# A two-layer relational graph attention kernel: the last eight products of layer 1 by column half, and the third part of W2 loaded in halves around them

## The chip, the cores and the metric

The kernel runs on one core of a Trainium2 chip. The core has a matrix engine (TensorE, in the profile PE, with its weight loads as PEld), a vector engine (VectorE, DVE), an engine for activations and copies (ScalarE, ACT), a general engine (GpSimd, POOL), and an engine that here only issues transfers (SyncE, SP). Sixteen DMA engines move data between the chip's memory (HBM) and the on-chip buffer (SBUF). SP, ACT and POOL each issue transfers on a queue of their own: SP the plain loads and stores, ACT the loads of W2, POOL the indirect gathers. Each engine works through its instructions in order, so an instruction that waits holds everything behind it on that engine.

The metric is device time in microseconds (us), the median of several runs. The profile is of one execution.

## The reference

Two layers of a relational graph attention network over 3125 nodes with 768 features and 53,125 edges sorted by target, with three relations; then a residual and a layer norm. Layer 1 has four heads, layer 2 one.

```python
def rgat_conv(x, W, q, k, b, src, dst, etype, heads, out_ch, n_nodes):
    xr = jnp.einsum('nd,rdf->rnf', x, W)
    oi = xr[etype, dst]
    oj = xr[etype, src]
    alpha = jax.nn.leaky_relu(oi @ q + oj @ k, NEG_SLOPE)
    m = jax.ops.segment_max(alpha, dst, num_segments=n_nodes)
    e = jnp.exp(alpha - m[dst])
    z = jax.ops.segment_sum(e, dst, num_segments=n_nodes)
    a = e / (z[dst] + EPS)
    msg = (a[:, :, None] * oj.reshape(-1, heads, out_ch)).reshape(-1, heads * out_ch)
    return jax.ops.segment_sum(msg, dst, num_segments=n_nodes) + b

h = jax.nn.elu(rgat_conv(x, W1, q1, k1, b1, src, dst, edge_type, 4, 192, n))
out = _layernorm(x + rgat_conv(h, W2, q2, k2, b2, src, dst, edge_type, 1, 768, n))
```

## The kernel before

The 3125 nodes are cut into 25 blocks of 128 (`NB` = 25, the last one partly empty), the 768 features into six tiles of 128 (`DT`) and two column halves of 384 (`HALF`). Products are made at full float32 precision from parts: each operand is split in a high and a low part, and three products (high by high, high by low, low by high) are added, so a block, a relation and a column half take 6 x 3 = 18 matrix products. The weights' parts lie in two buffers, `wH` and `wL`, of 18 feature tiles (three relations by six) by 770 columns: 384 columns of the first half, two more columns for attention, and 384 of the second half (`HW` = 386 is where the second half begins when they hold W2). The same buffers first hold W1 and then W2.

There are three phases and a preparation, in one hand-written order: the code's order is each engine's order, and only data and buffers make engines wait for one another.

**Phase 1** (`phase1`, L520) makes the products of layer 1 and the attention weights of all edges. Its steps n run over a list of 144 groups, a group being one block, one relation and one column half: 18 products by `d_group` (L688) into one of two `po` buffers of PSUM. `d_row` (L707) follows in the next step: ACT copies the group's result into a row buffer, and when both column halves are there, SP stores the row (128 x 772 numbers, 386 KB) into the table `tab1` in HBM. The row buffers are `share[0]` to `share[2]`, in turn. The first 120 groups go block by block (1 to 20); the last 24, for the blocks 21 to 24, go relation by relation, so that of each relation's weights the last reader comes early. In each relation the order is block by block, both halves of a block behind one another. So the groups 136 to 143 are relation 2 (the third), blocks 21 to 24, two halves each.

Beside the products, the edges' attention runs in steps that are tied to n: for every block, POOL issues 17 indirect gathers (tile `kt`, `a_gather`), and DVE, ACT and TensorE turn them into weights (`a_alpha` to `a_put`); the last block's steps lie behind the last product. W2 is also split into its parts in phase 1 (`w_split`) and written to HBM (`w2_d`).

`second_weights` (L508) brings one third (one relation) of W2 from `w2_d` into `wH` and `wL`, in four loads of 1152 KB on ACT's queue, each one column half of one buffer, and then fills the two attention columns with two small DVE instructions. It is a generator: each `next` issues one load, and the fifth one the DVE instructions. The thirds 0 and 1 are loaded in phase 1, at the steps m = 9 to 12 and 17 to 20, where m = n - 120. The third 2 is loaded in phase 2, since phase 1's last products still read W1 there.

**Phase 2** (`phase2`, L826) gathers `tab1`'s rows per edge, adds them up per node, and makes the products of layer 2. Its steps k run over the edge slots: `gather(k)` has POOL gather 128 rows (386 KB) into one of 14 buffers (`share[0]` to `share[8]` and five `g`); `high` makes the weighted selection masks on DVE (`selp`, L854); `sums` (L858) multiplies masks and rows on TensorE (`acc`, L876), for the first block in seven small batches and for all others in two. Behind a block's sums come its activation (`e_first` for the first block, `e_y`, `e_x`, `e_h` for the others), its transposition and split (`e_t`, `e_s`, `e_s2`: tile `hT`, L928 to L941), and its 18 `d_part` pieces of six products (L953) for three relations and two column halves, between the next block's sums; `d_row` (L956) copies and stores them into `tab2`. The third part of W2 is loaded at the steps 19, 20, 23 and 26, and its DVE instructions stand at step 28.

**Phase 3** (`phase3`, L1016) gathers `tab2`'s rows, and makes layer 2's attention, sums, residual and layer norm. Its gathers start when phase 2 has stored its last rows.

Of the kernel before, what the change touches and what calls it, by code (L numbers as in the profile page):

```python
# [54 lines left out]
def kernel(  # L55
# [21 lines left out]
    R = layers[0]["W"].shape[0]  # L77
    E = src.shape[0]
    NB = (N + P - 1) // P
# [4 lines left out]
    H1 = l1["H"]  # L84
    F1 = D // H1
# [5 lines left out]
    CW = F1 + 1  # L91
    LL = FRONT + E + BACK
    NK = (NB - 1) * SL + SLF
    V, S, G, T = nc.vector, nc.scalar, nc.gpsimd, nc.tensor
# [406 lines left out]
    def x_load(pre, b, to=None):  # L501
        n = min(P, N - b * P)
        xs[b] = pre.tile([P, D], F32, name="xr", bufs=1) if to is None else to[:, :D]
        if n < P:
            V.memset(xs[b], 0.0)
        nc.sync.dma_start(xs[b][:n], x[b * P:b * P + n, :])

    def second_weights(r, wH, wL):  # L508

        i = slice(r * DT, (r + 1) * DT)  # L510
        w = w2_d[r * DT * P:(r + 1) * DT * P, :].rearrange("(i p) (s c f) -> p s i c f", p=P, s=2, c=2)
        for c in range(2):
            for s, o in ((0, wH), (1, wL)):
                nc.scalar.dma_start(o.bitcast(F32)[:, i, c * HW:c * HW + HALF], w[:, s, :, c])
                yield
        V.tensor_copy(wH[:, i, HALF:HW], wkq2[:, i])
        V.tensor_sub(wL[:, i, HALF:HW], wkq2[:, i], wH[:, i, HALF:HW].bitcast(F32))


    def phase1(pre, work, psum, wH, wL, qq):  # L520
# [4 lines left out]
        rows = share[:3]  # L525
# [144 lines left out]
        def d_turn(b):  # L670
            xr = xs.pop(b)
            xt[b] = work.tile([P, 2, DT, P], F32R, **spare.get(b, dict(name="xT", bufs=2)))
            pt = psum.tile([P, 2, 512], F32, name="px", bufs=1)
            for t in range(DT):
                T.transpose(pt[:, t // 3, (t % 3) * P:(t % 3 + 1) * P], xr[:, t * P:(t + 1) * P], ident)
            p3 = pt[:, :, :3 * P]
            st["x", b] = xr, p3
# [25 lines left out]
            st["po", b, r, c] = po  # L703

        n_rows = []

        def d_row(b, r, c):  # L707
            po = st.pop(("po", b, r, c))
            if c == 0:
                n_rows.append(b)  # L710
            o = rows[len(n_rows) % 3]
            to = o.rearrange("p (h f) -> p h f", h=H1)[:, 2 * c:2 * c + 2, :F1]
            S.copy(to, po[:, :HALF].rearrange("p (h f) -> p h f", h=2))  # L713
            if c == 1:
                nc.sync.dma_start(
                    tab1[b * P * R:(b + 1) * P * R, :].rearrange("(p r) f -> p r f", r=R)[:, r, :], o)
                if b == 1:

                    nc.sync.dma_start(tab2[N * R:, :].rearrange("(p r) f -> p r f", r=R)[:, r, :], o)
# [53 lines left out]

        GB = NB - 4
        groups = [(b, r, c) for b in range(1, GB) for r in range(R) for c in range(2)]
        groups += [(b, r, c) for r in range(R) for b in range(GB, NB) for c in range(2)]
        ev = {}

        chain = ((-6, a_index), (-6, a_index2), (-5, a_gathers), (-5, a_next), (-4, a_next2))
# [12 lines left out]
        for b in range(2, GB + 1):  # L792
            for d, f, o in ((-8, d_turn, 0), (-7, d_split, 0), (-7, x_next, 1)):
                ev.setdefault(6 * b + d, []).append((f, NB - 1 if f is x_next and b == GB else b + o))
        for n in range(max(ev) + 1):
            for f, b in ev.get(n, ()):
                f(b)
            b, i = divmod(n, 6)
            if n == 2:
                nc.sync.dma_start(share[3][:, :D], x[:P, :])  # L800
            if n == 8:
                V.tensor_add(share[4][:, :D], share[3][:, :D], b2r)
                nc.sync.dma_start(xb_d[:P, :], share[4][:, :D])
            m = n - 6 * (GB - 1)
            if m in (1, 3, 5):
                d_turn(GB + 1 + m // 2)
                d_split(GB + 1 + m // 2)

            if m in (-8, -3):
                x_load(pre, GB + 1 + (m + 8) // 5, share[6 if m == -8 else 3])  # L810
            if m in (9, 17):
                w2s = second_weights(m // 16, wH, wL)
            if 9 <= m < 25:
                next(w2s, None)
            if 2 <= b < 2 + R * DT:
                if i == 0:
                    w_load(b - 2)
                if i == 2:
                    w_split(b - 2)
            if n < len(groups):  # L820
                d_group(n, *groups[n])
            if 0 < n <= len(groups):
                d_row(*groups[n - 1])


    def phase2(work, psum, wH, wL):  # L826
        bias1 = work.tile([P, D], F32, name="fbias1", bufs=1)
        nc.sync.dma_start(bias1, l1["b"][None, :].to_broadcast([P, D]))
        last_w2 = second_weights(R - 1, wH, wL)
        gs = share + [work.tile([P, RW], F32, name=f"g{i}", bufs=1) for i in range(5)]  # L830
        NG = len(gs)
        rows = [work.tile([P, RW], F32, name=f"r2_{i}", bufs=1) for i in range(3)]
# [148 lines left out]
        for i, b in enumerate(order):  # L981
# [5 lines left out]
            for m in range(6 * R):  # L987
                rc = divmod(m // 3, 2)
                k = e + m * SL // (6 * R) if i else first + 5 + m * (SL + 3) // (6 * R)
# [4 lines left out]
        for k in range(max(ev) + 1):  # L994
            if k < NK:
                gather(k)
            if k in (19, 20, 23, 26, 28):
                next(last_w2, None)
            if 0 <= k - LAG < NK:
                sums(k - LAG)  # L1000
            if k == first:
                e_first(order[0])
            if 0 <= k - LAG + 2 < NK:
                high(k - LAG + 2)
            for f, a in ev.get(k, []):
                f(*a)
            if k == NK + LAG:
                for b in range(len(xbs)):
                    x_load3(b)
# [299 lines left out]
    with tc.manual_schedule():  # L1309
        with tc.tile_pool(name="share", bufs=1) as pool:  # L1310
            share = [pool.tile([P, RW], F32, name=f"share{i}") for i in range(9)]

            two = pall.rearrange("p b j h -> p (b j h)")
            xbs = [t[:, :D] for t in share] + [two[:, i * D:(i + 1) * D] for i in range(2)]
            with tc.tile_pool(name="wbuf", bufs=1) as wbuf:
                wH = wbuf.tile([P, R * DT, D + 2], F32R, name="wH")
                wL = wbuf.tile([P, R * DT, D + 2], F32R, name="wL")
                with tc.tile_pool(name="pre", bufs=1) as pre:
                    qq = pre.tile([P, NB, H1, R], F32, name="qq")
                    with tc.tile_pool(name="work0", bufs=1) as work, tc.tile_pool(  # L1320
                        name="psum0", bufs=1, space=PSUM
                    ) as psum:

                        bank = psum.tile([P, 512], F32, name="bank")
                        bits = prepare(work, bank, share[8], share[6].bitcast(BF))

                        def more(n):
                            for _ in range(n):
                                next(bits, None)

                        buf = Buffers()
                        buf.go()
                        kqr = work.tile([P, DT, 2, H1], F32, name="kqr", bufs=1)
                        for s, name in ((0, "k"), (1, "q")):
                            nc.scalar.dma_start(kqr[:, :, s, :], l1[name].rearrange("(t p) h -> p t h", p=P))
                        more(1)
                        wk, kqs = (work.tile([P, DT, P], F32R, name=n) for n in ("wk", "kqs"))

                        def edges_ready():
                            more(100)  # L1340
                            a_load(pre, 0)

                        turns = nodes_kq(buf, pre, work, psum, bank, wk, kqs, wH, wL, qq, more, edges_ready)
                        weights_kq(buf, work, psum, bank, kqr, wk, kqs, wH, wL, next(turns), more)
                        next(turns)
                    with tc.tile_pool(name="work1", bufs=1) as work, tc.tile_pool(
                        name="psum1", bufs=1, space=PSUM
                    ) as psum:
                        phase1(pre, work, psum, wH, wL, qq)
                with tc.tile_pool(name="work2", bufs=1) as work, tc.tile_pool(name="psum2", bufs=1, space=PSUM) as psum:  # L1350
                    phase2(work, psum, wH, wL)
            with tc.tile_pool(name="work3", bufs=1) as work, tc.tile_pool(name="psum3", bufs=1, space=PSUM) as psum:
                phase3(work, psum)
    return nc.values_load(flag, min_val=0, max_val=1 << 24)
# [537 lines left out]
```

## Time and profile before

| what | value |
|---|---|
| runs | 2060.18 us median of 3 (2058.1 to 2061.2) |
| the profiled execution | 2060.05 us |
| its span, first to last instruction | 2058.3 us |
| mean granted TensorE clock | 0.915 |
| PE busy | 1761.5 us (86%) |
| POOL busy | 1327.4 us (64%) |
| DVE busy | 1185.0 us (58%) |
| ACT busy | 374.1 us (18%) |
| layer 1's last product ends (phase 1) | about 681 us |
| first row gather of phase 2 is issued | 693.92 us |
| phase 2's last product ends | about 1471.4 us |

Times inside the execution are microseconds from the start of the span. An engine's busy time counts what it computes, not what it waits for and not the issuing of transfers; those of ACT and SP are shown as ACTq and SPq. "Releaser" is what ended a wait. The chain that ended last is followed back from the last instruction of the program: at each step to what released it, or to the instruction before it on its engine. Idle time of an engine costs nothing unless it lies on that chain.

### The profile page before, as it was taken

Reading aid. Unit: us, or ns where it says so; the run is one execution under the profiler, and the core shown is the slowest. Engines: PE = TensorE matmul, PEld = TensorE weight load, DVE = VectorE, ACT = ScalarE, POOL = GpSimd, SP = SyncE. Lnnn points to the kernel's source line nnn. Section 1 sums busy time; section 2 is a strip of 40 time slices with the busy share of each in tenths; the row PEclk is TensorE's granted clock in tenths of the full one; section 3 lists DMA queues with packets and bytes.
Section 4 is the critical chain, followed back from the end, with each engine's and each line's share of the span. In section 5 each row is a group of like instructions: output and inputs, shape, how many; then the busy total and the mean of one; then the engine's idle time right before and its main releaser. Section 6 shows DMA issues by size and latency. Waiting matters only on the chain.

```text
span 2058.3 us, 41812 instructions
## 1 busy us (share of the span) xinstructions
PE 1761.5 (86%) x15027; PEld 1482.8 (72%) x15027; DVE 1185.0 (58%) x4163; ACT 374.1 (18%) x659; POOL 1327.4 (64%) x1326
## 2 busy tenths in 40 slices
PE   6989998999999579999999999999666766776775
PEld 5979998899899368988898888888523433433433
DVE  6545554555454456776677667666356556556654
ACT  5421211222111011111111111111102112112111
POOL 4257777777777745556555655564277777777773
PEclk9999999999999889999999999999877777787787
DMA  7655554555547687778777877876699999999993
GB/s 194 192 140 167 176 189 139 172 160 180 176 153 233 216 311 252 258 264 286 250 264 271 279 261 257 280 267 206 223 313 329 343 339 330 339 328 320 320 328 133
DMA packets 156844, 506.31 MB, mean 246 GB/s; under 512 B 43875, under 2 KB 57069, under 8 KB 156628
## 3 DMA queue, kind: packets, MB, share of 16 engines
q0 software_dynamic: 81904, 331.52, 48.2%
q1 hardware_dynamic: 62926, 156.02, 21.8%
q10 hardware_dynamic: 11798, 16.00, 2.3%
q8 instruction: 122, 2.00, 0.4%
q14 instruction: 94, 0.77, 0.1%
HBM read 412.55 MB, written 95.69 MB: 247 GB/s over the span
## 4 chain that ended last, share of the span: by engine, by line
PE 55%; issue 15%; POOL 14%; DMA 10%; DVE 5%; ACT 1%; POOLq 0%; ACTq 0%; DVEq 0%; SPq 0%
PE po L953 23%; PE acc L876 11%; POOL kt L462 11%; PE acc L1147 10%; PE po L698 4%; DMA G<-ftab,ridx 4%; POOL G L462 3%; DMA kt<-kt,ridx 2%; DMA wL<-w_d 2%; PE bank L285 1%; PE pt L263 1%; PE po L395 1%; PE pt L928 1%; DVE F L1107 1%; PE bc L1054 1%
## 5 line engine op out<-in xcount | busy, mean ns | idle before, releaser
L953 PE MATMUL po<-wH,hT 128*128 128x386 f32 (+1 forms) x1800 | 486.7, 345 | 8.5 <-DMA wH<-w_d 5.9
L462 POOL DMA_INDIRECT kt<-kt,ridx x374 | 395.5, 1057 | 114.0 <-issue 110.9
L698 PE MATMUL po<-wH,xT 128*128 128x384 f32 x1584 | 440.6, 348 | 9.7 <-ACT share L713 4.4
L462 POOL DMA_INDIRECT G<-ftab,ridx x374 | 374.2, 1001 | 114.0 <-issue 91.2
L854 DVE TENSOR_SCALAR selp<-frow,fdl,pall 128x32 f32<-128x32 f32 (+1 forms) x1688 | 381.1, 322 | 0.0
L953 PEld LDWEIGHTS po<-wH,hT 128*128 128x128 f32 x1800 | 331.7, 190 | 24.4 <-issue 21.0
L462 POOL DMA_INDIRECT share<-ftab,ridx x239 | 238.4, 997 | 169.8 <-PE acc L876 125.6
L953 PE MATMUL po<-wL,hT 128*128 128x386 f32 (+1 forms) x900 | 306.7, 341 | 4.8 <-DMA wL<-w_d 4.8
L698 PEld LDWEIGHTS po<-wH,xT 128*128 128x128 f32 x1584 | 294.7, 192 | 15.4 <-ACT share L713 6.2
L1147 PE MATMUL acc<-G,selp 128*32 128x386 f32 x2388 | 290.0, 582 | 2.9 <-DVE selp L1133 1.5
L698 PE MATMUL po<-wL,xT 128*128 128x384 f32 x792 | 270.3, 341 | 0.0
L1147 PEld LDWEIGHTS acc<-G,selp 128*32 128x32 f32 x2388 | 178.3, 128 | 77.3 <-issue 45.9
L462 POOL DMA_INDIRECT g<-ftab,ridx x135 | 135.7, 1005 | 108.3 <-PE acc L876 83.0
L876 PE MATMUL acc<-share,selp 128*32 128x193 f32 x3208 | 185.3, 330 | 2.7 <-DMA share<-ftab,rfirst 1.3
L961 ACT COPY r<-po 128x386 f32<-128x386 f32 (+1 forms) x150 | 72.3, 482 | 592.9 <-PE po L953 581.6
L953 PEld LDWEIGHTS po<-wL,hT 128*128 128x128 f32 x900 | 171.3, 190 | 5.2 <-DMA wL<-w_d 5.2
L1060 DVE TENSOR_SCALAR sT<-bc,cols 128x512 bf16<-128x512 f32 (+1 forms) x125 | 83.4, 667 | 150.6 <-PE bc L1054 147.9
L876 PEld LDWEIGHTS acc<-share,selp 128*32 128x32 f32 x3208 | 125.7, 111 | 44.0 <-issue 7.7
L698 PEld LDWEIGHTS po<-wL,xT 128*128 128x128 f32 x792 | 151.7, 191 | 0.0
L1054 PE MATMUL bc<-d,one 1*128 1x512 bf16 (+1 forms) x125 | 48.5, 388 | 85.2 <-DVE sT L1060 82.1
L713 ACT COPY share<-po 128x384 f32<-128x384 f32 x144 | 67.8, 477 | 275.2 <-PE po L698 268.2
L876 PE MATMUL acc<-g,selp 128*32 128x193 f32 x1768 | 115.0, 328 | 1.6 <-DMA g<-ftab,rfirst 1.2
(262 smaller groups left out, 1911.5 us busy)
## 6 DMA issues: line engine op xcount, KB each, us to landing
ftab<-share SPq DMA_DIRECT2D x75, 386.0 KB
ftab<-r SPq DMA_DIRECT2D x75, 386.0 KB
share<-in_L_gnn_W_dram SPq DMA_DIRECT2D x36, 384.0 KB
w_d<-w2hl SPq DMA_DIRECT2D x18, 768.0 KB
sT<-dr_d SPq DMA_DIRECT2D x25, 544.0 KB
share<-in_x_dram SPq DMA_DIRECT2D x27, 384.0 KB
xb_d<-share SPq DMA_DIRECT2D x25, 384.0 KB
xr<-in_x_dram SPq DMA_DIRECT2D x21, 384.0 KB
```

Source lines behind the costliest of these rows:

```text
L263: T.transpose(pt[:, f, c * P:(c + 1) * P], a[:, (2 * i + f) * P:(2 * i + f + 1) * P], ident)
L285: T.matmul(to, a[:, 2 * i + f, :], t[:, f, :w], start=(n == 0), stop=(n == 2 * DT - 1))
L462: return G.indirect_dma_start(out=to, out_offset=None, in_=tab, in_offset=_index(i[:, j:j + 1]), bounds_check=NP * R - 1, oob_is_err=False)
L698: m = T.matmul(po[:, :HALF], xT[:, s, t, :], w[:, i, sl], start=(n == 0), stop=(n == 3 * DT - 1))
L713: S.copy(to, po[:, :HALF].rearrange("p (h f) -> p h f", h=2))
L854: V.tensor_scalar(sel[:, h, :hi - lo], row[:, lo:hi], dl[:, b, j:j + 1], pall[:, b, j, h:h + 1], op0=ALU.is_equal, op1=ALU.mult)
L876: T.matmul(acc[32 * t:32 * t + 32, h // 2, c], sel[:, h, 32 * (t - WINDOW[i][0]):][:, :32], g[:, h * CW:(h + 1) * CW], start=(i == u[0] an ...
L953: T.matmul(po[:, :wd], hT[:, k, t, :], w[:, r * DT + t, sl], start=(t == 0 and n == 0), stop=(t == DT - 1 and n == 2))
L961: S.copy(o[:, c * HW:c * HW + wd], po[:, :wd])
L1054: T.matmul(bc[:, :n], one, s["d"][:, 4 * i * P:4 * i * P + n], start=True, stop=True)
L1060: V.tensor_scalar(s["sT"][:, 4 * i * P:4 * i * P + n], bc[:, :n], cols[:, b:b + 1], None, op0=ALU.is_equal)
L1147: T.matmul(acc[32 * t:32 * t + 32, c, :HW], st[b, j][:, 32 * (t - WINDOW[j][0]):][:, :32], gs[:, (base(b) + j) % NG, c * HW:(c + 1) * HW], ...
```

## The change

The last eight groups, 136 to 143, are put in another order: first the first column half of the blocks 21, 22, 23 and 24, then the second half of the four. For that, four rows are open at once, and the fourth one (block 24) gets `share[3]`, whose four columns of ones are set by a small DVE instruction.

The four loads of W2's third part, which overwrite the weights these groups read, move from phase 2 into phase 1: the first column half of `wH` and of `wL` at m = 21 and m = 22, that is behind the copies of groups 139 and 140 on ACT; the second half of both behind the copy of group 143, the last one. The two DVE instructions of the attention columns move from step 28 of phase 2 to step 19.

```diff
         n_rows = []
+        row_of = {}
 
         def d_row(b, r, c):
             po = st.pop(("po", b, r, c))
             if c == 0:
                 n_rows.append(b)
-            o = rows[len(n_rows) % 3]
+                row_of[b, r] = rows[len(n_rows) % 3] if (b, r) != (NB - 1, R - 1) else share[3]
+                if (b, r) == (NB - 1, R - 1):
+                    V.memset(share[3].rearrange("p (h f) -> p h f", h=H1)[:, :, F1:CW], 1.0)
+            o = row_of[b, r]
...
         groups = [(b, r, c) for b in range(1, GB) for r in range(R) for c in range(2)]
-        groups += [(b, r, c) for r in range(R) for b in range(GB, NB) for c in range(2)]
+        groups += [(b, r, c) for r in range(R - 1) for b in range(GB, NB) for c in range(2)]
+        groups += [(b, R - 1, c) for c in range(2) for b in range(GB, NB)]
...
+        last_w2 = second_weights(R - 1, wH, wL)
         for n in range(max(ev) + 1):
...
             if 9 <= m < 25:
                 next(w2s, None)
+            if m in (21, 22):
+                next(last_w2)
...
             if 0 < n <= len(groups):
                 d_row(*groups[n - 1])
-
-
-    def phase2(work, psum, wH, wL):
+            if n == len(groups):
+                next(last_w2)
+                next(last_w2)
+        return last_w2
+
+
+    def phase2(work, psum, wH, wL, last_w2):
...
-        last_w2 = second_weights(R - 1, wH, wL)
...
-            if k in (19, 20, 23, 26, 28):
+            if k == 19:
                 next(last_w2, None)
...
-                        phase1(pre, work, psum, wH, wL, qq)
+                        last_w2 = phase1(pre, work, psum, wH, wL, qq)
...
-                    phase2(work, psum, wH, wL)
+                    phase2(work, psum, wH, wL, last_w2)
```

## The prediction

> **What bounds the kernel now.** The profiled execution took 2060.05 us, of which 2058.3 are the span; the median of the runs is 2060.18, so sums made against 2060.05 stand 0.13 below it. I read the chain that ended last first, in order of time, around the end of layer 1's products (about 680 us) and the start of phase 2:
>
> ```profile
> 704.35 5.79 DMA share<-ftab,rfirst
> 710.86 4.56 DMA g<-ftab,rfirst
> 721.93 42.87 DMA wL<-w_d
> 768.10 5.64 PE po L953 x30
> ...
> 786.50 5.39 PE acc L876 x100
> 791.89 5.47 PE po L953 x30
> ...
> 798.11 5.29 PE po L953 x30
> 803.40 4.08 PE acc L876 x96
> ```
>
> Columns: start, length, what. Row gathers lead to about 720; then one transfer, a piece of W2, holds the chain for 42.87 us; after that TensorE's own work follows without a hole, and windows of 100 us from 800 to 1400 show PE busy 100.00 at clock 1.00. So a microsecond won before 768 is kept to the end of phase 2, and phase 3's gathers start when that ends. What the load costs TensorE is in its timeline:
>
> ```profile
> 753.12 0.34 PE L953 MATMUL po<-wH,hT 128*128 128x386 f32 x1
> 759.37 0.66 PE L953 MATMUL po<-wH,hT 128*128 128x384 f32 x1 [5.92 <-DMA wH<-w_d]
> 764.85 0.69 PE L953 MATMUL po<-wL,hT 128*128 128x384 f32 x1 [4.81 <-DMA wL<-w_d]
> ...
> 773.67 2.84 PE L876 MATMUL acc<-share,selp 128*32 128x193 f32 x64
> ```
>
> The 386-wide products are the first column half and found their weights there; the 384-wide ones, second half of the third part, waited 5.92 + 4.81 us. They then run at 0.66 to 0.69 us where the others take 0.34: the clock had fallen. Next the stretches by window (PE, PEld, DVE, ACT, POOL busy, then PE clock, DMA share, GB/s):
>
> ```profile
> 664.00:676.00 12.00, 11.91 (x83) 11.60 (x82) 3.62 (x19) 1.44 (x4) 9.26 (x10) 1.00 1.05 371
> 676.00:693.00 17.00, 4.55 (x39) 4.00 (x39) 4.73 (x10) 1.15 (x3) 13.04 (x14) 0.72 0.19 46
> 694.00:720.00 26.00, 14.91 (x181) 9.10 (x182) 18.59 (x81) 1.35 (x3) 19.90 (x21) 0.81 0.87 294
> 720.00:753.00 33.00, 30.15 (x295) 25.93 (x296) 22.35 (x98) 3.57 (x6) 22.90 (x23) 0.84 1.01 380
> ```
>
> The loads of the third part stand in the full stretch, 720 to 753, beside the row gathers; from 676 to 693 the DMA engines are nearly idle. What sets the start of phase 2 is POOL, which issues attention gathers (kt) and then row gathers in one line of 1.3 us steps:
>
> ```profile
> 692.62 1.00 POOL L462 DMA_INDIRECT kt<-kt,ridx  x1 [0.30 <-issue]
> 693.92 1.00 POOL L462 DMA_INDIRECT share<-ftab,rfirst  x1 [0.30 <-issue]
> ```
>
> and ACT, whose queue carries the loads:
>
> ```profile
> 680.06 0.46 ACT L713 COPY share<-po 128x384 f32<-128x384 f32 x1
> ...
> 721.93 11.68 ACTq L514 DMA_DIRECT2D wL<-w_d  x1
> 733.65 0.48 ACT L961 COPY r<-po 128x386 f32<-128x386 f32 x1 [11.33 <-PE acc L876]
> ```
>
> 680.06 is the copy of the last product, so TensorE and the table stores are done some 12 us before POOL needs them. The fourth load of a row held ACT's queue for 11.68 us.
>
> **The change, part by part.**
>
> *Wait removed.* In a settled block, the time from the end of one batch of sums to the start of the next is 803.40 - (786.50 + 5.39) = 11.51 us. Here the batch before the wait ended at 748.96 and the next began at 773.67: 24.71 us. With the weights there I take the settled pattern: 24.71 - 11.51 = **13.20 us** won, which is 10.73 us of waiting and 2.47 us of slow clock and of the one product between the two waits. The other inputs of the batch then due at 760.5 are there: its last row gather (the twelfth after POOL resumed at 733.64) is issued at 747.96, and the longest landing in the chain above is 5.79 us, so 753.8. DVE has done its masks for it in the settled pattern too.
>
> *Loads moved.* Four quarters of 1152 KB (1.18 MB), 4.72 MB. Copies of groups 139, 140 and 143 on ACT end at 666.3, 670.1 and 680.5 now; the loads stand right behind these: first column half at 666.3 and 670.1, second half, both, at 680.5. The last three loads of W2's second part are issued 661.3 to 662.5 and ride the same queue; the window 664 to 676 shows them with two table stores at 371 GB/s, done at about 676 (4.33 MB / 0.371 = 11.7 us). Behind them: 4.72 MB and the last two stores, 0.79 MB, 5.51 MB in all, at 371 GB/s 14.9 us, so all lands at about **691**. TensorE's first use of the first half is at 750.3, of the second at 753.3. Cover: the idle stretch 676 to 693; the last kt gather is issued at 692.62, the first row gather at 693.92, so the margin is 1.6 to 2.9 us. Cost taken: 0. Without the cover, bounds follow under the rivals.
>
> *Issues and queues.* On ACT the two early loads stand ahead of the copies of groups 140 and 141, which are due at 669.66 and 672.85: each issue takes 0.37 to 0.48 us where the queue is free, and 3 us lie open. If it is held (three loads are in flight at 666.3), TensorE has two po buffers and the products may end up to 11 us later before a store is late for 693.92. The last two loads hold nobody: ACT's next work is the exponential at 698.43. In phase 2 ACT loses the hold of 11.68 us, which hid under TensorE's work (PE ran on at 731.86).
>
> *Reordered groups.* The same 144 groups of 18 products. Four table stores now leave after groups 140 to 143 (670.2, 673.3, 676.5, 680.5) where they left after 137, 139, 141 and 143; SP has only one small load queued behind them, issued at 681.11 and used at 696. Row buffers: group 138's copy (662.43) reuses the row stored at 651.73, 10.7 us before, with the DMA engines nearly idle at 660; group 139 uses share[3], whose memset costs DVE about 0.06 us, the length of such a memset at L834, while DVE waits 11.96 us for kt anyway. Cost 0.
>
> *Two DVE copies.* L516 and L517 (0.16 and 0.17 us) move from step 28, where DVE was waiting, to step 19, ahead of the hT subtraction (L941, 724.03) on which TensorE waited 1.65 us. On the path: **+0.33 us**. Bounds: 0 to 0.7, if the clock doubles it for TensorE.
>
> Sum: 2060.05 - 13.20 + 0.33 = **2047.2 us**.
>
> **A rule against the shared transfers.** The last table store is issued at 680.5 with 4 MB of loads ahead of it or around it; if it were served in order of issue it would land near 691. The Trainium skill, "DMA: Bandwidth & Descriptors", section "Queues, rings and completion order", says each DMA engine takes turns between the queues that have work, a packet at a time. By that rule the store (on SP's queue) lands in a few microseconds, whatever ACT's queue holds, while each kt gather waits turns behind load packets. No row here gives the landing of one store beside such loads. By either reading the sum stays 2047.2; the rule lowers the chance of the third rival.
>
> **Rivals.**
> 1. *The loads run into the row gathers.* For it: beside gathers the four loads took 718.91 to 764.80, 4.72 MB in 45.9 us, only 103 GB/s. Against: no row gathers run from 676 to 693. If loads and stores moved at 250 GB/s, they would end at 676 + 22 = 698, with 1.1 MB left at 693.9; that delays the fourteenth gather by 1.1/0.38 = 2.9 us at most. The last kt gather under load: a landing of 3.81 us stands in the chain at 660.46, 2.13 us at the idle 692.62, so 1.7 us more. Time 2050 to 2052.
> 2. *The halves are not free of each other*, so that a second-half product waits for a first-half load (same tile). Group 141 would wait for the first load (679.5), 142 for the second (682.7); the products would end at 689, the last store near 692, and the last 2.36 MB run into the gathers: +0.6 for the start and about 3 us for the transfers, 2051. Against: the two column ranges don't meet.
> 3. *Slower: ACT held by the two early loads.* Such a hold is in the trace (11.68 us). Each hold delays the copy behind it, TensorE fills both po buffers and stops, and the last store and the first row gather go late. Two holds of 11.68: the copy of 140 at 678.1, of 141 at 690.3, the last store at 694.6; landing takes 2.36 us (the last store of layer 2, 1472.02), so gathers start 3 us late, and 2.36 MB collide with them, 6 us: 2056. It decides when the store leaves after 704.4, where the gathers start 12.9 us late, that is with holds of some 17 us each; with holds of 23 us, 2080. Against: 680.5 leaves the last loads behind all copies, and the three loads ahead drain at 371 GB/s, 3 us each.
> 4. *The wait is hidden anyway*: another input of the 760.5 batch is late. It would need a gather or a mask later by over 7 us than now: 2057 to 2060.
>
> **How the numbers follow.** Forecast 0.76 (2044 to 2050: the runs before spread over 3.1 us, and the unknown costs 0 to 2 us), rival 1 0.10, rival 2 0.03, rival 3 0.07 (0.05 of it slower than before), rival 4 0.04. The range 2044 to 2053 holds the forecast and the first two rivals. About 0.2%, 4.1 us, can be told from no change here. Faster by more: 0.76 + 0.10 + 0.03 and a little of rival 3, 0.90; within: rival 4 and some of 3, 0.05; slower: 0.05.
>
> **What would show it.** Right: no wait of a 384-wide product on wH or wL near 753, the first three batches of phase 2 about 11.5 to 17 us apart, DMA share well above 0.19 from 676 to 691, the first row gather still at 693.9, PE busy without a hole from 725 on. Wrong: a row gather that starts after 695, ACT copies of groups 140 to 142 later than 670, 673 and 676, products that wait for a load, or phase 2 ending later than 1459 (1471.5 now).

## The result and the profile after

The changed kernel takes 2047.93 us, the median of runs from 2046.48 to 2049.07. The kernel before, measured beside it, takes 2060.69 us (2058.1 to 2064.93). The ratio is 0.9936, with a 95% interval from 0.9923 to 0.9948: 0.64% faster, and 12.8 us between the medians. The prediction was 2047.2 us. Six of the experiments below fell where the kernel before itself took 2677 or 2745 us instead of 2060; each ratio is against the kernel before beside it.

The profiled execution after took 2048.89 us, of which 2047.1 are the span. Products that stood in line 953 of the kernel before stand in line 964, and the sums of line 876 in line 887. First, the chain that ended last in the changed kernel, in order of time (start, length, what):

```profile
692.91 0.52 POOL kt L462
...
696.50 4.09 DMA kt<-kt,ridx
...
708.23 6.40 DMA share<-ftab,rfirst
714.75 4.74 DMA g<-ftab,rfirst
...
729.39 5.74 PE po L964 x22
735.13 4.08 PE acc L887 x96
739.22 7.61 PE po L964 x42
746.83 5.39 PE acc L887 x104
752.22 5.48 PE po L964 x30
757.70 0.66 PE pt L939 x6
758.36 5.31 PE po L964 x30
763.66 4.08 PE acc L887 x96
```

The row gathers still lead to the first block. Behind them stood a transfer of W2 for 42.87 us; now TensorE's own work follows piece on piece. The pattern around the old wait has closed up: batch to 752.22, products to 763.66 with one transposition between, the next batch. From the end of that batch to the next are 11.44 us, where the settled pattern in the kernel before has 11.51.

TensorE's waits between 640 and 780 us in the changed kernel (what waited, for what, us in total, how often, the longest) have no line for wH or wL; the four longest are:

```profile
PE pa L642 <- DVE al L636: 18.7, 3, 17.1
PE pt L939 <- DVE ey L927: 3.2, 2, 2.8
PE pa L659 <- ACT e L655: 2.5, 1, 2.5
PE po L964 <- DVE hT L952: 2.1, 1, 2.1
```

The 384-wide product that waited 5.92 us in the kernel before now runs with the row of 386-wide ones. TensorE's timeline in the changed kernel (start, busy time, what):

```profile
756.30 0.51 PE L964 MATMUL po<-wH,hT 128*128 128x386 f32 x2
756.66 0.34 PE L964 MATMUL po<-wL,hT 128*128 128x384 f32 x1
756.83 0.51 PE L964 MATMUL po<-wH,hT 128*128 128x384 f32 x2
```

No bracket with a wait stands behind these lines, and 0.34 us is the price at full clock, where it was 0.66 to 0.69.

Where the loads went is in the windows of the changed kernel (PE, PEld, DVE, ACT, POOL busy, then PE clock, DMA share, GB/s):

```profile
684.00:688.00 4.00, 0.25 (x11) 0.14 (x6) 1.75 (x4) 0.28 (x1) 3.09 (x4) 1.00 0.93 317
688.00:692.00 4.00, 0.00 (x0) 0.00 (x0) 0.00 (x0) 0.00 (x0) 3.09 (x4) 0.57 1.06 387
692.00:696.00 4.00, 0.00 (x0) 0.00 (x0) 0.00 (x0) 0.00 (x0) 3.08 (x4) 0.50 0.61 186
696.00:700.00 4.00, 0.00 (x0) 0.00 (x0) 0.00 (x0) 0.00 (x0) 3.09 (x4) 0.50 0.23 55
...
730.00:755.00 25.00, 25.00 (x280) 21.93 (x279) 15.28 (x70) 2.78 (x5) 17.21 (x18) 0.94 0.85 290
```

The once idle stretch is full to about 694.5 (0.61 of the four us from 692), and the DMA engines are nearly idle again when the first row gather is issued at 697.80. In the stretch from 730 to 755, where the loads had stood, their share is 0.85 and no longer 1.03.

The two profiled executions differ by 11.16 us, and the sum of the pieces between fixed points is:

| stretch | before | after | difference |
|---|---|---|---|
| start to the exponential ahead of the change's first instruction | 661.34 | 664.65 | +3.31 |
| from there to the first row gather | 32.58 | 33.15 | +0.57 |
| first row gather to the first transposition of phase 2 | 25.94 | 26.14 | +0.20 |
| first transposition to the second block of products | 5.17 | 5.45 | +0.28 |
| to the first batch of the next block | 6.83 | 5.67 | -1.16 |
| first batch to the second | 11.71 | 11.70 | -0.01 |
| second batch to the first batch of the block behind | 30.10 | 16.84 | -13.26 |
| the rest of phase 2 | 697.76 | 697.83 | +0.07 |
| from there to the end of the execution | 588.62 | 587.46 | -1.16 |

The line of -13.26 is the change. The +3.31 in front is not: over eight profiled kernels with the same code up to there, but for the order of one or two products, this exponential starts between 659.57 and 664.65, and between 661.34 and 664.46 in the five of them that have the old order. The +0.57 lies within what these eight differ by from the exponential to the first row gather (32.12 to 33.15 us). The -1.16 of the second block of products comes of the 6.83 in the kernel before, the longest of the eight; the others take 5.67 to 6.36.

### The profile page after: what moved, and what is told of

Its sections match the earlier page's. It is cut to its first block, busy times and chain, and to the rows that moved or that the text cites. A ratio compares the mean times of both kernels' runs of the same rounds, so it can differ in the third digit from the quotient of the medians.

```text
span 2047.1 us, 41815 instructions
## 1 busy us (share of the span) xinstructions
PE 1753.3 (86%) x15027; PEld 1477.1 (72%) x15027; DVE 1184.6 (58%) x4164; ACT 373.9 (18%) x659; POOL 1330.1 (65%) x1326
## 4 chain that ended last, share of the span: by engine, by line
PE 57%; POOL 14%; issue 14%; DMA 8%; DVE 5%; ACT 1%; POOLq 0%; ACTq 0%; DVEq 0%; SPq 0%
PE po L964 24%; PE acc L887 11%; POOL kt L462 10%; PE acc L1158 9%; PE po L698 5%; POOL G L462 4%; DMA G<-ftab,ridx 3%; DMA kt<-kt,ridx 2%; PE bank L285 1%; PE pt L263 1%; PE po L395 1%; PE pt L939 1%; DVE F L1118 1%; PE acc L1170 1%; PE bc L1065 1%
```

## The experiments

The theory: the whole gain is the wait of the second-half products on W2, and any way that has the loads landed before their use without pushing the row gathers is worth the same. The rivals put a part of the gain in the new order of the groups, or a price on ACT's queue or on the gathers. One table first, from the profile of each kernel measured where the kernel before takes about 2060 us. "Gather to transposition" is from the first row gather of phase 2 to the first transposition, the stretch in which gathers delayed by loads would show. Where the second column gives a span, it runs from the first issue to the end of the last one. Each ratio is against the kernel before measured beside that run (2059.05 to 2060.69 us), so the ratios compare the rows better than the medians do.

| kernel | the four loads are issued at | gather to transposition, us | wait on W2, us | median, us | ratio, 95% interval |
|---|---|---|---|---|---|
| before | 718.9, 719.3, 721.5, 721.9 (held to 733.6) | 25.94 | 10.73 | 2060.69 | 1 |
| the change | 669.1, 673.0, 683.8, 685.3 | 26.14 | 0 | 2047.93 | 0.9936 (0.9923 to 0.9948) |
| all four behind the products | 683.3 to 689.9 | 26.29 | 0 | 2047.35 | 0.9939 (0.9922 to 0.9955) |
| second half in phase 2 | 667.3, 671.1, 722.2, 722.6 | 25.80 | 0 | 2046.66 | 0.9943 (0.9922 to 0.9963) |
| all four at the first steps | 699.3 to 718.2 | 30.56 | 0 | 2050.97 | 0.9960 (0.9946 to 0.9975) |
| five steps earlier | 700.1 to 707.6, 725.4 | 30.78 | 0 | 2050.98 | 0.9958 (0.9944 to 0.9972) |
| loads twice | 664.1 to 707.0 | 32.02 | 0 | 2052.61 | 0.9965 (0.9953 to 0.9976) |
| five steps later | 722.7, 723.1, 731.3, 738.8 | 26.05 | 12.66 | 2061.08 | 1.0002 (0.9992 to 1.0012) |

**The new order alone.** The groups in the new order, with the loads at their old steps:

```diff
 (the change, but in phase 1)
-            if m in (21, 22):
-                next(last_w2)
-            if n == len(groups):
-                next(last_w2)
-                next(last_w2)
 (and in phase 2)
-            if k == 19:
+            if k in (19, 20, 23, 26, 28):
```

> Only the new order of the last eight groups; the four loads of W2's third part stay at the steps 19, 20, 23 and 26 of phase 2. Theory A (the gain is the 13.2 us that TensorE lost to the second-half loads near 753 us): the wait is back, 2059 to 2062 us, two waits of a 384-wide product of 5 to 6 us each. Theory C (the order itself is worth or costs something): 2 us or more away from the kernel before.

> The kernel of e1 once more: only the new order of the last eight groups, the four loads at the steps 19, 20, 23 and 26 of phase 2. Where the kernel before takes about 2060 us. Theory A: the wait of the 384-wide products is back at 10 to 12 us in all, 2059 to 2062 us. Theory C (the order itself is worth or costs something): 2 us or more away from the kernel before.

Measured: 2679.06 us beside 2677.0 of the kernel before (ratio 1.0008, 0.9977 to 1.0040), and the second time 2748.44 beside 2745.15 (1.0007, 0.9989 to 1.0025). Neither trace has a wait of TensorE on wH or wL, although the loads stand at their old place, so the disputed wait isn't there to be removed or kept. These runs say that the order costs nothing there, and nothing about the wait. Whether the order alone moves the time where the kernel before takes 2060 us wasn't measured. What the other traces have of it: from the exponential named in the table to the copy of layer 1's last product, five profiles in the old order take 18.72 to 19.25 us, and three in the new order 19.03 to 19.16.

**All four loads behind the products, in the old order.** If the halves matter, this loses; if only the wait does, it is worth the same:

```diff
 (the kernel before, and)
+            if n == len(groups):
+                for _ in range(4):
+                    next(last_w2)
...
-            if k in (19, 20, 23, 26, 28):
+            if k == 28:
```

> The old order of groups, no load before the end of the products: all four loads of the third part right behind the last copy on ACT, the two small DVE instructions at step 28 as before. Theory A: 4.72 MB at about 370 GB/s are 12.8 us from the last copy, so they end about when the first row gather is issued; no wait on W2 in phase 2, 2047 to 2049 us, no different from the changed kernel by more than 1 us. Theory C (halves and early loads are needed, since the loads otherwise run into the last kt gathers and the first row gathers): 2051 to 2055 us.

> The kernel of e2 once more: old order of groups, all four loads of the third part right behind the last copy, the two DVE instructions at step 28. In e2's execution TensorE, ACT and DVE waited for no visible reason again and again (the time before was 2677 us there), so that no kernel met the wait that is in question. Where the kernel before takes about 2060 us. Theory A: the loads end 12.8 us behind the last copy, at about the first row gather; no wait on W2, 2047 to 2049 us. Theory C (halves and early loads are needed): 2051 to 2055 us, the first row gather or the last kt gather late by 4 us or more.

Measured: 2047.35 us, 0.9939 (0.9922 to 0.9955), the same as the change. Beside a kernel before of 2677.0 us it took 2688.38 (1.0044, 1.0017 to 1.0071), 0.4% more, and its trace shows where such a loss comes from. The small load of the last block's window (102 KB on SP's queue, issued at 958.19, while the four large ones go out on ACT's from 957.12 on) is what DVE's scan waits for, and the chain of that execution runs through it:

```profile
977.90 0.95 DVE L650 TENSOR_TENSOR_SCAN share<-w,pa 68x384 f32<-68x384 f32 x1 [18.16 <-DMA w<-ed_d]
```

From its issue to the scan are 19.7 us; with no loads there, in the traces of the new order alone and of the first steps beside the same 2677 us, they are 7.4 and 7.2, with waits of 5.78 and 5.60; the scan comes some 12 us later than it would. In the run of 2047 us the same small load is issued at 684.53 and the scan, at 702.99, doesn't wait for it, because the last block's attention comes later there. So the place behind the last product is free only as long as nothing small that is needed soon stands beside the loads. In the run of 2047 us they also reach into the first row gathers, issued from 697.35. Its windows:

```profile
688.00:692.00 4.00, 0.00 (x0) 0.00 (x0) 0.00 (x0) 0.00 (x0) 2.99 (x3) 0.55 1.04 386
692.00:696.00 4.00, 0.00 (x0) 0.00 (x0) 0.00 (x0) 0.00 (x0) 2.99 (x3) 0.50 1.06 350
696.00:700.00 4.00, 0.00 (x0) 0.00 (x0) 0.00 (x0) 0.00 (x0) 3.03 (x4) 0.50 1.09 348
```

Full to 700, where the change was done by 694.5; yet the gathers lead to the transposition in 26.29 us, 0.15 more than after the change. So neither the new order, nor the halves, nor the two early loads are needed for the gain: all four loads fit behind the last product.

**Half of the move.** The first column half early as in the change, the second half in phase 2, at the steps 23 and 26:

```diff
 (the change, but in phase 1)
-            if n == len(groups):
-                next(last_w2)
-                next(last_w2)
 (and in phase 2)
-            if k == 19:
+            if k in (23, 26, 28):
                 next(last_w2, None)
```

> The changed kernel, but the second column half is loaded in phase 2, at the steps 23 and 26. Theory A with the shared rate seen before (103 GB/s for the loads beside row gathers): 2.36 MB take 23 us from about 722 to 726, landing 745 to 749 us, ahead of the 753 to 757 us at which TensorE first needs them; no wait, 2047 to 2049 us: halving what is moved in phase 2 is enough. If the rate is not what decides (the wait hangs on where the second half is loaded, theory C): the waits of about 11 us return, 2056 to 2060 us.

> The kernel of e3 once more: first half early as in the changed kernel, second half in phase 2 at the steps 23 and 26. Where the kernel before takes about 2060 us. Theory A with 103 GB/s for loads beside row gathers: the second half lands at 745 to 749 us, before its first use at 753 to 757; no wait on W2, 2047 to 2049 us. Theory C: the waits return, 2056 to 2060 us.

Measured: 2046.66 us, 0.9943 (0.9922 to 0.9963), with no wait on wH or wL, and beside 2677.0 us no difference (0.9997, 0.9970 to 1.0023). The two late loads are issued at 722.2 and 722.6 and share full DMA engines (1.02 from 730 to 750) with the gathers, but there are two of them and not four, and they are in before their products. Taking 2.36 MB out of that stretch is enough.

**All four loads at the first steps of phase 2.** No new order, no move into phase 1; the loads simply ride beside the first row gathers:

```diff
-            if k in (19, 20, 23, 26, 28):
+            if k in (0, 1, 2, 3, 28):
                 next(last_w2, None)
```

> The kernel before, with the four loads at the steps 0 to 3 of phase 2, behind the last exponential on ACT (about 699 us), so that all 4.72 MB run beside the row gathers of block 0. Theory A (row gathers keep their 1.3 us steps beside loads, as they did from 734 to 753): the loads land by 699 + 46 = 745 us, before 750; no wait, the first batches late by 0 to 3 us, 2047 to 2051 us. Theory B (the transfers' collision is the price, and the idle stretch is what the change is worth): block 0's rows come late by 5 to 10 us, 2053 to 2058 us.

> The kernel of e4 once more: old order, all four loads at the steps 0 to 3 of phase 2, behind the last exponential on ACT, so beside the row gathers of block 0. Where the kernel before takes about 2060 us. Theory A (only the late second half costs; row gathers keep their 1.3 us steps beside loads): no wait on W2, from the first row gather to the first transposition of block 0 26 to 29 us (25.9 before), 2047 to 2050 us. Theory B (the idle stretch behind the products is what the change is worth, since loads beside block 0's gathers hold these up): 31 us or more from the first row gather to the first transposition, 2052 to 2058 us.

Measured: 2050.97 us, 0.9960 (0.9946 to 0.9975): 9.3 us faster than the kernel before beside it, where the change won 12.8 (beside 2677.0 us: 0.9991, 0.9964 to 1.0019). The time and the stretch of 30.56 us fall between what the two theories expected the second time. The wait is gone, and a part of it is paid back at the gathers. The chain of this kernel:

```profile
698.72 5.89 DMA share<-ftab,rfirst
704.61 0.14 issue
704.74 1.52 PE acc L876 x22
...
711.75 9.15 DMA g<-ftab,rfirst
```

The gather that ends the first block's wait lands after 9.15 us, where it took 4.56 in the kernel before, although POOL issues on in steps of 1.3 us. That is 4.6 us, and so much longer is the stretch from gather to transposition (30.56 against 25.94). 13.3 won and 4.6 paid give 8.7; measured were 9.3. This is the price of missing the idle stretch: 4.6 us with the loads beside the first block's gathers. That the gathers are stretched but not held until the loads are done fits what the Trainium skill says in "DMA: Bandwidth & Descriptors", section "Queues, rings and completion order": each DMA engine takes turns, a packet at a time, between the queues that have work; no row here shows when each load landed, so the run agrees with the rule and doesn't prove it.

**Five steps earlier.** A point between, to see what the time of issue alone does:

```diff
-            if k in (19, 20, 23, 26, 28):
+            if k in (14, 15, 18, 21, 28):
                 next(last_w2, None)
```

> The kernel before with its four loads five steps earlier, at the steps 14, 15, 18 and 21. Theory D, formed after e9: from the first load on the DMA engines are full (about 400 GB/s), row gathers take what they ask for, and the loads land when loads and gathers together have been moved; starting 6.5 us earlier helps only by the room that the gathers leave there (294 of 400 GB/s from 694 to 720: 0.1 MB per us, 0.7 MB, 1.7 us): waits of about 9 us, 2057 to 2060 us. A fixed share of 103 GB/s for the loads: they land 6.5 us earlier, waits of about 4 us, 2052 to 2055 us.

> The kernel of e11 once more: the kernel before with its four loads five steps earlier, at the steps 14, 15, 18 and 21. Where the kernel before takes about 2060 us. Theory D (the DMA engines are full, the loads land when loads and gathers together have been moved): only the room left by the gathers helps, 1.7 us; waits of about 9 us, 2057 to 2060 us. A fixed share of 103 GB/s for the loads: landing 6.5 us earlier, waits of about 4 us, 2052 to 2055 us.

Measured: 2745.72 beside 2745.15 (0.9993, 0.9979 to 1.0007), then 2050.98, 0.9958 (0.9944 to 0.9972). The second lies outside what either theory expected, and the timeline tells why: the experiment wasn't what it was meant to be. ACT has nothing between its exponential at 700.06 and its next activation at step 18, so the first three loads went out at 700.07, 700.48 and 701.08, as early as in the experiment before, and not five steps ahead of the old place. The stretch from gather to transposition, 30.78, repeats its price, 4.8 us, and with three loads in it instead of four, since the last one is issued only at 725.38. So the price isn't one per byte of the loads.

**Five steps later.** The loads further behind, to see whether the wait grows by the delay:

```diff
-            if k in (19, 20, 23, 26, 28):
+            if k in (24, 25, 28, 31, 33):
                 next(last_w2, None)
```

> The kernel before with its four loads five steps later, at the steps 24, 25, 28 and 31, the DVE instructions at 33. Theory A with a shared rate (the loads take what the row gathers leave, about 46 us for four): the wait grows by about the delay of the issue, 5 steps of 1.3 us: 6 to 7 us more, 2066 to 2068 us, and the waits of the 384-wide products sum to 16 to 18 us; if the first half is late too, a 386-wide product waits as well. If the wait hangs on something other than when the loads begin: 2060 us.

Measured: 2061.08 us, 1.0002 (0.9992 to 1.0012): no difference, where theory A expected 2066 to 2068. TensorE's timeline in this kernel has the two waits again:

```profile
763.40 0.66 PE L953 MATMUL po<-wH,hT 128*128 128x384 f32 x1 [9.58 <-DMA wH<-w_d]
767.14 0.69 PE L953 MATMUL po<-wL,hT 128*128 128x384 f32 x1 [3.08 <-DMA wL<-w_d]
```

12.66 us of waiting against 10.73, two us more. The third load was issued at 731.30 and not at 721.53, 9.8 us later; the product that needs it starts 4.0 us later (763.40 against 759.37). The fourth is off ACT's queue at 739.12, where the hold let it go at 733.61, 5.5 us later; its product starts 2.3 us later (767.14 against 764.85). So the landing moved by less than half of the issue, and 1.3 us of that are only the later start of this execution's row gathers (695.23 against 693.92). Two windows of the kernel before, then the same two of this one, show what sets the landing:

```profile
730.00:755.00 25.00, 23.45 (x274) 20.05 (x273) 15.03 (x64) 3.26 (x6) 16.57 (x18) 0.98 1.03 396
755.00:760.00 5.00, 0.63 (x1) 0.29 (x1) 0.98 (x6) 0.00 (x0) 0.47 (x1) 0.85 1.04 408
```

```profile
730.00:755.00 25.00, 23.82 (x279) 20.40 (x277) 15.52 (x67) 3.25 (x6) 17.29 (x19) 0.99 1.03 398
755.00:760.00 5.00, 0.00 (x0) 0.00 (x0) 1.37 (x8) 0.00 (x0) 0.85 (x1) 0.76 1.04 408
```

The DMA engines are full in both until 760, some five us after POOL's last gathers (754.47 and 754.85; then POOL waits 20 and 22 us for TensorE to release buffers). In the five us from 760 their share is 0.41 and 0.81, so they are done near 762 and 764. Loads and gathers together are a fixed sum of bytes, and both kernels are through with it at nearly the same time. In this pair of profiles the last landing hangs on all that the DMA engines have to move more than on when the loads are issued; the run five steps earlier, meant as a second point, doesn't give one.

**The loads doubled.** The change, with all four loads issued once more behind the last two; the copies write the same numbers again, so that only transfers are added:

```diff
             if n == len(groups):
                 next(last_w2)
                 next(last_w2)
+                again = second_weights(R - 1, wH, wL)
+                for _ in range(4):
+                    next(again)
```

> The changed kernel with all four loads of the third part issued a second time behind the last two (same data, same place): 4.72 MB more in and behind the idle stretch. Theory A: the second set ends at about 691 + 4.72 MB / 0.37 = 704 us or later, as it waits for the first set to land, so it runs some 10 us beside the first row gathers; these keep their steps, the first transposition comes 0 to 3 us later, no wait on W2: 2047 to 2051 us. Theory B: 5 to 10 us lost, 2053 to 2058 us.

Measured: 2052.61 us, 0.9965 (0.9953 to 0.9976); 7.7 us faster than the kernel before beside it, where the change won 12.8, and between the two theories, neither of which had the cause. Lines of the timeline of this kernel, from ACT, DVE and POOL:

```profile
691.53 5.78 ACTq L514 DMA_DIRECT2D wH<-w_d  x1
697.40 9.60 ACTq L514 DMA_DIRECT2D wL<-w_d  x1
700.14 0.29 DVE L654 TENSOR_TENSOR e<-pa,share 68x128 f32<-68x128 f32 x1
707.05 0.31 ACT L655 ACTIVATE e<-e 68x128 f32<-68x128 f32 x1 [27.97 <-issue]
708.06 0.99 POOL L462 DMA_INDIRECT g<-ftab,rfirst  x1 [4.03 <-PE pa L659]
```

DVE has the last block's exponents at 700.43. ACT takes them at 707.05, 6.6 us later, because its queue stands in the issue of two loads, 5.78 and 9.60 us long. DVE waits 7.40 us for the weights that come of it and POOL 4.03 us before its next row gather, and the stretch from gather to transposition grows from 26.14 to 32.02. One of the second loads lands at 707.95, just as DVE and POOL go on (707.83 and 708.06), and the profile's chain runs through that landing; so the late exponential is shown, but not that the landing by itself would have cost nothing. The mechanism of the slower rival is real: a held queue of ACT delays what is behind it, and the place is the exponential and not the copies.

## Why the prediction was right

The time was 0.7 us from the forecast, and the gain 12.8 us where 12.85 were forecast. The mechanism is the one forecast, but so close a hit is partly luck: the pieces from the exponential to the end of phase 2 sum to 13.31 us won, since 0.77 us lost before the first transposition and 1.16 won in the second block of products stood nowhere in the sum and nearly cancel. Point by point:

- **The wait removed** was put at 13.20 us from the gap of a settled block; it was 13.26. To take the settled gap for the new one, and not only the 10.73 us of waiting, brought in 2.5 us of slow clock and of the product between the two waits, and those came.
- **The loads moved at cost 0** held. The loads ended 10.2 us behind the end of the last copy (684.3 to about 694.5) where 10.5 had been worked out from the copy at 680.06 (the last product ends at 679.8, not at about 681 as in the table of times), at 387 GB/s in the full window where 371 were taken. The margin to the first row gather was 3.3 us; to the last kt gather, issued at 696.50, it was 2.0. One row moved: the last kt gather took 4.09 us in the chain where it took 2.13 before, with the DMA engines at 0.23 from 696 to 700. The first rival had priced just this, at 1.7 us; it came to 1.96, and only 0.20 of it is left at the transposition. Why the gather is slower with the loads already in is open.
- **ACT's queue** was put at no cost, with holds in the range, and held nobody. ACT's timeline in the changed kernel shows the two early loads behind the copies, with the holds that were feared:

```profile
669.13 0.48 ACT L717 COPY share<-po 128x384 f32<-128x384 f32 x1 [2.91 <-PE po L698]
669.14 2.17 ACTq L514 DMA_DIRECT2D wH<-w_d  x1
672.94 0.48 ACT L717 COPY share<-po 128x384 f32<-128x384 f32 x1 [3.33 <-PE po L698]
672.95 2.27 ACTq L514 DMA_DIRECT2D wL<-w_d  x1
676.10 0.48 ACT L717 COPY share<-po 128x384 f32<-128x384 f32 x1 [2.68 <-PE po L698]
```

  They are 2.2 and 2.3 us long, less than the 3.2 to 3.8 us from one product's copy to the next, and each copy still waits for TensorE's product and not for the queue.
- **The DVE copies** cost 0.28 us on the path, 0.33 were taken.
- **The order of the groups and the stores** were put at nothing. No row after contradicts that, and all four loads behind the products in the old order take the same time; by itself, beside a kernel before of 2060 us, the order wasn't measured.
- **The signs.** Three that the prediction called wrong appear by the clock of the execution: the first row gather starts at 697.80 and not before 695, the copies of the groups 140 to 142 start at 672.94, 676.10 and 679.32, and phase 2 ends at 1461.4, later than 1459. All three carry the 3.31 us that this execution was late before the change began. Counted from the exponential, the copies start within 0.06 us of their old place and phase 2 ends 13.3 us earlier. The signs should have been given from such a fixed point.

Where the working was off, without moving the sum: the rival of loads that run into the row gathers took 103 GB/s as what loads get beside gathers, and 2.9 us for 1.1 MB left over. The DMA engines were full at 396 GB/s there, loads and gathers together; four loads beside the first gathers cost 4.6 us and three cost 4.8, where 4.72 and 3.54 MB by the rival's reckoning (1.1 MB at 380 GB/s) would be 12.4 and 9.3, and where the four loads were issued behind the products, the piece that reached into the gathers cost 0.15. The slower rival had its mechanism right and its place wrong: it looked at the early loads, where the holds are some 2 us, and let the last two "hold nobody", which is so only because there are two. With four more behind them the exponential waits 6.6 us. By the rule of turns the prediction had a store land in a few microseconds whatever ACT's queue holds; for small loads on the same queue the traces say otherwise: the one issued at 662.83 in the kernel before, beside three loads of W2, holds DVE's scan until 677.75, and the one beside four loads took 19.7 us (above). The store itself was in within 7.4 us there: the first row gather, which reads its rows, starts at 965.02, and the copy ahead of the store ends at 957.59. The sum didn't rest on it. The 1.16 us that the clock gave in the second block of products had no term either, and aren't the change's: with the loads still in phase 2, five steps later, this block takes 5.79 us, against 5.67 after and 6.83 in the kernel before (below).

## What to carry to other kernels

When a load waits beside gathers on full DMA engines, count the bytes that must be moved before the use rather than the time of issue: here, in one pair of profiles, issues 5.5 and 9.8 us later brought uses only 2.3 and 4.0 us later, and taking half of the load's bytes into an idle stretch won as much as taking all of them. The value of removing a stall is read from the same gap in a settled block, not from the wait alone, since the slow clock and the work caught between two waits come back with it. A stretch in which the DMA engines are idle is free only if nothing needed soon is loaded in it: one small load beside the four large ones landed so late that the run lost 0.4%. A transfer put on a computing engine's queue can hold it; look for the first thing that this engine must compute behind the last one, and try the move with the transfers doubled.

## What the runs showed of the hardware

- **Issuing a load can hold the engine's queue.** An issue of a 1152 KB load on ACT took 0.37 to 0.57 us for the first two in a row; a third or later one in a short time took anything from 0.37 to 12.22 us, mostly over 2 (5.61 and 12.22 at the first steps of phase 2, 11.68 in the kernel before, 9.60 with the loads doubled). With the loads doubled an exponential stood behind it for 6.6 us.
- **The DMA engines moved up to 408 GB/s** of loads and gathers, over stretches of 5 to 25 us. The Trainium skill, "DMA: Bandwidth & Descriptors", section "Specifications", gives about 358 GB/s as the limit from HBM to one core, half of what two cores share. Here one core ran, and the windows from 730 to 760 us (396 to 408, with some row stores among them) are above that; the measurement decides here.
- **The clock comes back after a variable time.** From the start of the second block of products on, TensorE works without a hole; the granted clock is back at 1.00 after 3.6 us in the changed kernel (729.39 to 733.0) and after 6.1 us in the kernel before (725.03 to 731.1), and with it the 1.16 us of the table. In the six other profiles of the table of experiments it takes 3.7 us in five and 5.0 in one.
- **A small load beside large ones lands late.** The 102 KB load of a block's window, on SP's queue, took 7.2 and 7.4 us from issue to use with no loads of W2 beside it, 14.9 us beside three of them (662.83 to 677.75 in the kernel before) and 19.7 beside four.
- **Work that the change doesn't touch moves by microseconds between executions**: the exponential near the end of phase 1 starts 5.1 us apart over eight profiles. A single profile's total therefore can't be compared to a microsecond; pieces between fixed points can.
